# One block for all self-attention scores, and both experts in one strided stationary read

## The chip, the cores and the metric

The kernel runs on one core of a Trainium2 chip. The metric is the device time of one execution in microseconds. Five engines work side by side: TensorE (PE in the profile; its weight loads are listed apart as PEld), VectorE (DVE), ScalarE (ACT), GpSimd (POOL) and SyncE (SP), which issues most of the transfers. TensorE writes to PSUM, which has eight banks of 512 float32 values on each of 128 partitions; the operands of its matmuls lie in SBUF.

## The reference

The input is 16 batches of 128 tokens by 512 values, and for each batch a context of 2048 rows by 512. All is float32.

```python
x = x + xattn(layernorm(x), ctx)     # softmax(h @ ctx.T) @ ctx, over the 2048 rows
x = x + attn(layernorm(x), ...)      # 16 heads of 32, causal, 128 tokens
x = x + ffn(layernorm(x), ...)

# attn: q = [q_c, rope(q_e)], k likewise, v; each projected down to 16 x 64 and up to 16 x 32
scores = einsum("bhqd,bhkd->bhqk", q, k) / sqrt(32)
att = softmax(where(causal, scores, -inf))
y = einsum("bhqk,bhkd->bhqd", att, v) @ Wc

# ffn: two of eight experts for each batch, chosen by its first token
gates = softmax(top2(x[:, 0] @ Wr.T))          # zero for the other six
mid = einsum("blh,erh->belr", x, A)            # rank 64 for each expert
out = x + einsum("be,belr,ehr->blh", gates, mid, Bw)
```

## The kernel before

The 16 batches are worked through one after another, and each has four stages written as generators: `score` (the cross-attention scores and their exponentials), `attend` (those weights times the context), `inner` (the self-attention) and `experts` (the feed-forward part). Each `yield` ends a step. A loop over `b` calls `step(kind, batch, n)` in an order written out by hand, so that steps of four different batches alternate: `inner` of batch b, `experts` of b - 1, `attend` of b + 1, `score` of b + 2. The helpers `matmul` (line 84) and `transpose` (line 87) keep TensorE's instructions in that order. The other engines' instructions are ordered by the scheduler, from what they depend on. Loads in the loop are issued from SP's queue as their buffers come free; the gathers of expert weights and the outputs are issued from POOL.

The names on which the text rests:

- `score`: `psc` is a bank of 512 scores, four for a batch, each from four matmuls of 128 rows with 512 columns; line 214 copies it to `sc` and takes its maximum, and line 223 makes the exponentials of all 2048.
- `attend`: `tr_p` turns four 128 x 128 blocks of `sc` in PSUM, line 120 copies them to `pT` on ACT, and `av` accumulates the product with the context in one bank. Line 247 adds the input. Then a layer norm follows (lines 105 to 112; the power on line 110 is POOL's).
- `inner`: `q`, `k` and `v` are products with weights folded at the start; `tr_q` and `trk` turn q and k. Line 298 makes `kb`, two copies of 128 columns of the turned k, with a mask that leaves one head of 32 partitions in each 64-partition half. `pss` holds the scores of four heads in one bank: a matmul contracts over 64 partitions and gives two heads, 256 columns. Line 316 adds the causal mask, line 322 takes the maxima, line 323 scales them, line 325 makes the exponentials head by head with their sums, and lines 329 and 330 normalise. `tr_p_a` turns the weights, `y` multiplies them with v in 32-column pieces, line 352 copies the result to `yT`, and `o` multiplies that with `Wc`.
- `experts`: DVE works out the two experts from `lg`, POOL gathers their weights to `wa` (two gathers, one row of 1 KB to each partition for each expert, line 400) and `wb` (line 405); `mid` is the first product, line 424 scales it by the gates, and `ffn` is the second product.

PSUM's eight banks are shared out by three pools: `ps_tr` (three, for what is turned), `ps_sc` (two, for `psc` and `pss`) and `ps_acc` (three, for `q`, `k`, `v`, `av`, `y`, `mid`, `o`, `ffn`).

In `inner` of the kernel before, the scores are made in two steps of eight heads. Each takes both banks of `ps_sc`, and steps of `attend` stand between and after the two. Every matmul is two records of the profile.

Of the kernel before, what the change touches and what calls it, by code (L numbers as in the profile page):

```python
# [11 lines left out]
F32 = mybir.dt.float32  # L12
I32 = mybir.dt.int32
U32 = mybir.dt.uint32
AF = mybir.ActivationFunctionType
ALU = mybir.AluOpType
AX = mybir.AxisListType
PSUM = bass.MemoryType.PSUM

P = 128  # L20
B, S, V, D = 16, 128, 2048, 512
H, L, DH = 16, 64, 32
DE = DH // 2
E, R = 8, 64
KC = D // P
VC = V // 512
HC = H // 4
TOP = 2
EPS = 1e-5
SCALE = 1.0 / math.sqrt(DH)  # L30
# [3 lines left out]
C_ID, C_MASK, C_COS, C_SIN, C_BLK = 0, 128, 256, 272, 288  # L34
# [26 lines left out]
def perceiver_block(ctx: ExitStack, tc: tile.TileContext, io: dict, out: bass.AP):  # L61
    nc = tc.nc
# [20 lines left out]
    def matmul(*args, **kwargs):  # L83
        tc.keep_in_program_order(nc.tensor.matmul(*args, **kwargs))  # L84
# [12 lines left out]
    def bank(pool, tag, name):  # L97
        return pool.tile([P, 512], F32, tag=tag, name=name)
# [152 lines left out]
    def inner(b):  # L251

        x1, h = firsts.pop(b)
        hT = p1.tile([P, KC, S], F32, tag="hT2", name=f"hT2_{b}")
        transposed(h, hT, f"2_{b}")
        yield

        qk = p1.tile([P, 2, D], F32, tag="qk", name=f"qk_{b}")
        vv = p1.tile([P, D], F32, tag="vv", name=f"vv_{b}")
        for i, n in enumerate(("q", "k", "v")):  # L260
            ps = bank(ps_acc, "acc", f"{n}_{b}")
            for c in range(KC):
                matmul(ps, hT[:, c, :], w[n][:, c, :], start=(c == 0), stop=(c == KC - 1))
            nc.scalar.copy(vv if n == "v" else qk[:, i, :], ps)
            if n == "k":

                e = qk.rearrange("p i (h f) -> p (i h) f", f=DH)[:, :, DE:]
                turned = p1.tile([P, 2 * H, DE], F32, tag="turned", name=f"turned_{b}")
                for odd in range(2):
                    nc.gpsimd.tensor_tensor(  # L270
                        turned[:, :, odd::2],
                        e[:, :, 1 - odd :: 2],
                        cst[:, None, C_SIN + odd : C_SIN + DE : 2].to_broadcast([P, 2 * H, DE // 2]),
                        ALU.mult,
                    )
                nc.vector.tensor_tensor(
                    e, e, cst[:, None, C_COS : C_COS + DE].to_broadcast([P, 2 * H, DE]), ALU.mult
                )
                nc.vector.tensor_tensor(e, e, turned, ALU.add)
            yield  # L280

        qT = p1.tile([P, HC, S], F32, tag="qT", name=f"qT_{b}")
        transposed(qk[:, 0, :], qT, f"q_{b}")
        trk = bank(ps_tr, "tr", f"trk_{b}")
        for c in range(HC):
            transpose(trk[:, c * P : (c + 1) * P], qk[:, 1, c * P : (c + 1) * P], ident)
        yield
        att = p1.tile([P, H, S], F32, tag="att", name=f"att_{b}")
        nmx = p2.tile([P, H], F32, tag="nmx", name=f"nmx_{b}")
        sm = p2.tile([P, H], F32, tag="sm", name=f"sm_{b}")  # L290
        rsm = p2.tile([P, H], F32, tag="rsm", name=f"rsm_{b}")
        for two in range(2):

            pss = [bank(ps_sc, "sc", f"pss_{b}_{two}_{half}") for half in range(2)]
            kbs = []
            for c in (2 * two, 2 * two + 1):
                kb = p2.tile([P, 2, S], F32, tag="kb", name=f"kb_{b}_{c}")
                nc.vector.tensor_tensor(
                    kb,
                    trk[:, None, c * P : (c + 1) * P].to_broadcast([P, 2, S]),  # L300
                    cst[:, C_BLK : C_BLK + 2, None].to_broadcast([P, 2, S]),
                    ALU.mult,
                )
                kbs.append(kb)

            for i, kb in enumerate(kbs):
                for half, ps in enumerate(pss):
                    of = slice(half * 2 * DH, (half + 1) * 2 * DH)
                    matmul(
                        ps[:, i * 2 * S : (i + 1) * 2 * S],  # L310
                        qT[of, 2 * two + i, :], kb[of].rearrange("p h t -> p (h t)"),
                        start=True, stop=True,
                    )
            for half, ps in enumerate(pss):
                hs = slice(8 * two + 4 * half, 8 * two + 4 * half + 4)
                nc.vector.tensor_tensor(  # L316
                    att[:, hs, :],
                    ps.rearrange("p (h t) -> p h t", h=4),
                    cst[:, None, C_MASK : C_MASK + S].to_broadcast([P, 4, S]),
                    ALU.add,  # L320
                )
                nc.vector.tensor_reduce(nmx[:, hs], att[:, hs, :], AX.X, ALU.max)  # L322
                nc.vector.tensor_scalar_mul(nmx[:, hs], nmx[:, hs], -SCALE)  # L323
                for i in range(hs.start, hs.stop):
                    nc.scalar.activation(  # L325
                        att[:, i, :], att[:, i, :], AF.Exp,
                        bias=nmx[:, i : i + 1], scale=SCALE, accum_out=sm[:, i : i + 1],
                    )
                nc.vector.reciprocal(rsm[:, hs], sm[:, hs])
                nc.vector.tensor_tensor(  # L330
                    att[:, hs, :], att[:, hs, :], rsm[:, hs, None].to_broadcast([P, 4, S]), ALU.mult
                )
            yield

        flat = att.rearrange("p h t -> p (h t)")

        def heads(c):
            first = c // 2 * 8 + c % 2 * 2
            return first, first + 1, first + 4, first + 5

        now = [turn(flat, heads(c), f"a_{b}_{c}") for c in range(HC)]
        yield
        acc = bank(ps_acc, "acc", f"y_{b}")
        for c in range(HC):
            for j in range(4):
                at = c * P + j * DH
                matmul(
                    acc[j * DH : (j + 1) * DH, c * P : (c + 1) * P],
                    vv[:, at : at + DH], now[c][:, j, :], start=True, stop=True,
                )  # L350
        yT = p1.tile([P, HC, S], F32, tag="yT", name=f"yT_{b}")
        nc.scalar.copy(yT, acc.rearrange("p (c t) -> p c t", c=HC))  # L352
        yield
        acc = bank(ps_acc, "acc", f"o_{b}")
        for c in range(HC):
            matmul(acc, yT[:, c, :], w["c"][:, c, :], start=(c == 0), stop=(c == HC - 1))
        x2 = p2.tile([P, D], F32, tag="x2", name=f"x2_{b}")
        nc.vector.tensor_tensor(x2, acc, x1, ALU.add)
        lasts[b] = (x2, layernorm(x2, f"3_{b}"))
        yield  # L360

    def experts(b):
# [50 lines left out]
        nc.vector.tensor_scalar(gate, ex, column(C_TWO), column(C_ONE), ALU.mult, ALU.add)  # L413
        nc.vector.tensor_scalar(gate, gate, dn, None, ALU.mult)
        yield
        ps = bank(ps_acc, "acc", f"mid_{b}")
        for c in range(KC):
            for i in range(TOP):
                matmul(
                    ps[i * R : (i + 1) * R, :S], wa[:, i, c * R : (c + 1) * R], hT[:, c, :],  # L420
                    start=(c == 0), stop=(c == KC - 1),
                )
        mid = p2.tile([P, S], F32, tag="mid", name=f"mid_{b}")
        nc.scalar.activation(mid, ps[:, :S], AF.Copy, scale=gate)
        yield
# [13 lines left out]
    def step(kind, b, n=1):  # L439
        if not 0 <= b < B:  # L440
            return
        if (kind, b) not in gens:
            gens[kind, b] = kind(b)
        for _ in range(n):
            next(gens[kind, b])
# [40 lines left out]
    for b in range(B):  # L486
        if 2 < b + 2 < B:
            load_turned(b + 2)
        step(inner, b, 2)
        step(experts, b - 1)  # L490
        step(score, b + 2)
        step(inner, b)
        step(experts, b - 1)
        step(score, b + 2, 2)
        step(inner, b)
        step(score, b + 2)
        step(attend, b + 1)
        step(inner, b)
        step(attend, b + 1)
        step(inner, b)  # L500
        step(attend, b + 1)
        step(score, b + 2)
        step(attend, b + 1)
        if b == B - 1:

            step(experts, b - 1, 2)
        step(inner, b)
        step(attend, b + 1)
        if b + 2 < B:
            load_ctx(b + 2)  # L510
        if b + 3 < B:
            load_x(b + 3)
        step(inner, b)
        if b < B - 1:
            step(experts, b - 1)
        step(inner, b)
        step(inner, b + 1)
        if b < B - 1:
            step(experts, b - 1)
        step(score, b + 3)  # L520
# [43 lines left out]
```

## Time and profile before

| | |
|---|---|
| median of 3 runs | 910.48 us (910.23 to 912.07) |
| the profiled execution | 910.24 us |
| its span, first to last instruction | 908.5 us |
| mean granted TensorE clock | 0.983 |
| busy: PE, DVE, ACT, POOL | 873.1, 388.6, 291.0, 143.7 us |
| records of `pss`, count and busy time | 256, 38.6 us |
| records of `mid`, count and busy time | 256, 19.9 us |
| weight loads of `mid`, 64 columns, mean | 147 ns |

The span is the time between the first and the last instruction in one profiled execution, and the 1.7 us that are left of its 910.24 us lie around it. A row of the timeline gives the start, the length, the engine, the line, the operation, what it writes and reads, its shapes and how many records were merged. For TensorE, "128*64" before the shapes says that the stationary operand covers 128 rows and 64 columns of the array. The ends of matmuls are modelled, and records that run side by side overlap, so times on TensorE are best read from one start to the next.

### The profile page before, as it was taken

To read this page: it belongs to the slowest core of one execution; us is meant where nothing else is said; L and a number is where in the kernel's file an instruction comes from. 1 tells how busy PE (TensorE), PEld (TensorE's weight loads), DVE (VectorE), ACT (ScalarE), POOL (GpSimd) and SP (SyncE) were. 2 spreads that over 40 slices of the span, in tenths; PEclk is the share of its full clock that TensorE was granted. 3 is DMA by queue.
4 is the path that set the end of the run, shared out by engine and by line. 5 is a ranking of instruction groups with operands and counts; after the bars stand their busy time and mean duration, and the time that the engine had idled before them with its cause. 6 is when DMAs were issued, how large, how long until landed. Compare 5 with 4: busy or idle time off the path is not lost.

```text
span 908.5 us, 10128 instructions
## 1 busy us (share of the span) xinstructions
PE 873.1 (96%) x3600; PEld 445.2 (49%) x3600; DVE 388.6 (43%) x1020; ACT 291.0 (32%) x845; POOL 143.7 (16%) x214
## 2 busy tenths in 40 slices
PE   5999999999999999999999999999999999999972
PEld 2444545555455555545555554555555455555531
DVE  1132535344453534445353444545344454536251
ACT  1132422425142232514233151523315152334240
POOL 0000021120302112030211203021120302112212
PEclk9999999999999999999999999999999999999985
DMA  7997635546273554526356462735545262240011
GB/s 307 365 343 312 238 121 209 208 144 221 90 258 122 209 209 152 219 92 255 117 209 209 155 221 93 251 114 209 208 162 223 89 248 102 73 148 24 12 35 36
DMA packets 29394, 159.21 MB, mean 175 GB/s; under 512 B 4128, under 2 KB 4256, under 8 KB 12960
## 3 DMA queue, kind: packets, MB, share of 16 engines
q1 hardware_dynamic: 25248, 145.98, 43.8%
q0 software_dynamic: 4096, 12.59, 4.0%
q8 instruction: 29, 0.48, 0.2%
q14 instruction: 21, 0.17, 0.1%
HBM read 154.36 MB, written 4.19 MB: 175 GB/s over the span
## 4 chain that ended last, share of the span: by engine, by line
PE 95%; DVE 2%; issue 1%; ACT 1%; POOL 1%; DMA 0%; POOLq 0%; SPq 0%; ACTq 0%
PE av L84 25%; PE psc L84 25%; PE o L84 6%; PE q L84 6%; PE v L84 6%; PE k L84 6%; PE pss L84 4%; PE tr_p_a L87 3%; PE tr_p L87 3%; PE tr L87 2%; PE y L84 2%; PE mid L84 2%; PE ffn L84 1%; PE tr_q L87 1%; PE trk L87 1%
## 5 line engine op out<-in xcount | busy, mean ns | idle before, releaser
L84 PE MATMUL av<-ctx,pT 128*128 128x512 f32 x512 | 233.3, 598 | 0.2 <-ACT pT L120 0.2
L84 PE MATMUL psc<-ctxT,hT 128*128 128x512 f32 x512 | 232.2, 603 | 0.7 <-ACT hT L120 0.7
L84 PEld LDWEIGHTS av<-ctx,pT 128*128 128x128 f32 x512 | 93.4, 190 | 109.9 <-issue 104.8
L84 PEld LDWEIGHTS psc<-ctxT,hT 128*128 128x128 f32 x512 | 95.5, 193 | 104.7 <-issue 103.6
L325 ACT ACTIVATE att<-att,nmx 128x128 f32<-128x128 f32 x256 | 99.0, 388 | 82.7 <-DVE nmx L323 82.7
L214 DVE TENSOR_SCALAR_CACHE_REDUCE sc<-psc 128x512 f32<-128x512 f32 x64 | 44.2, 691 | 133.7 <-PE psc L84 132.8
L109 POOL TENSOR_SCALAR rs<-mv 128x1 f32<-128x1 f32 x48 | 10.4, 229 | 534.6 <-DVE mv L107 534.1
L84 PE MATMUL o<-w_c,yT 128*128 128x512 f32 x128 | 59.2, 605 | 1.5 <-ACT yT L352 1.5
L84 PE MATMUL q<-w_q,hT 128*128 128x512 f32 x128 | 58.8, 602 | 0.7 <-ACT hT L120 0.7
L84 PE MATMUL v<-w_v,hT 128*128 128x512 f32 x128 | 57.6, 592 | 0.0
L84 PE MATMUL k<-w_k,hT 128*128 128x512 f32 x128 | 57.5, 592 | 0.0
L112 DVE TENSOR_SCALAR h<-x,mv,rs 128x512 f32<-128x512 f32 x48 | 39.3, 819 | 39.7 <-POOL rs L110 38.8
L120 ACT COPY pT<-tr_p 128x512 f32<-128x512 f32 x64 | 35.2, 575 | 65.3 <-PE tr_p L87 65.2
L120 ACT COPY hT<-tr 128x512 f32<-128x512 f32 x48 | 27.0, 593 | 80.7 <-PE tr L87 80.7
L247 DVE SCALAR_TENSOR_TENSOR x<-av,rden,x 128x512 f32<-128x512 f32 x16 | 12.0, 750 | 89.5 <-PE av L84 89.5
L325 ACT ACTIVATION_READ_ACCUMULATOR att<-att,nmx 128x1 f32 x256 | 47.7, 186 | 0.0
L330 DVE TENSOR_TENSOR att<-att,rsm 128x512 f32<-128x512 f32 x64 | 44.1, 689 | 1.6
L223 ACT ACTIVATE sc<-sc,nm 128x2048 f32<-128x2048 f32 x16 | 32.0, 2002 | 35.8 <-DVE nm L221 35.8
L400 POOL DMA_INDIRECT wa<-in_A_dram,g_blocks x32 | 32.9, 1028 | 66.4 <-issue 48.5
L87 PEld LDWEIGHTS tr_p<-cst,sc 128*128 128x128 f32 x256 | 30.9, 141 | 24.8 <-issue 24.8
L316 DVE TENSOR_TENSOR att<-pss,cst 128x512 f32<-128x512 f32 x64 | 42.2, 681 | 1.7 <-PE pss L84 1.7
L322 DVE TENSOR_REDUCE nmx<-att 128x4 f32<-128x512 f32 x64 | 40.7, 675 | 0.0
(95 smaller groups left out, 859.1 us busy)
## 6 DMA issues: line engine op xcount, KB each, us to landing
ctxT<-in_ctxT_dram SPq DMA_DIRECT2D x64, 1024.0 KB, 5.1
ctx<-in_ctx_dram SPq DMA_DIRECT2D x64, 1024.0 KB, 4.8
x<-in_x_dram SPq DMA_DIRECT2D x16, 256.0 KB, 4.8
out_dram<-out POOLq DMA_DIRECT2D x16, 256.0 KB, 2.4
down_q<-in_Wq_downT_dram SPq DMA_DIRECT2D x2, 1024.0 KB, 9.5
down_k<-in_Wk_downT_dram SPq DMA_DIRECT2D x2, 1024.0 KB, 7.4
down_v<-in_Wv_downT_dram SPq DMA_DIRECT2D x2, 1024.0 KB, 8.3
w_c<-in_Wc_dram SPq DMA_DIRECT2D x1, 1024.0 KB, 13.5
```

The lines of the kernel that those rows point to most:

```text
L84: tc.keep_in_program_order(nc.tensor.matmul(*args, **kwargs))
L87: tc.keep_in_program_order(nc.tensor.transpose(*args))
L112: nc.vector.tensor_scalar(h, src, mv[:, 0:1], rstd, ALU.subtract, ALU.mult)
L120: nc.scalar.copy(dst, tr.rearrange("p (c t) -> p c t", c=4))
L214: nc.vector.tensor_scalar(sc[:, v * 512 : (v + 1) * 512], ps, 1.0, None, ALU.mult, ALU.max, accum_out=mx[:, v : v + 1],)
L223: nc.scalar.activation(sc, sc, AF.Exp, bias=nm, accum_out=den)
L247: nc.vector.scalar_tensor_tensor(x1, acc, rden, xs.pop(b), ALU.mult, ALU.add)
L316: nc.vector.tensor_tensor(att[:, hs, :], ps.rearrange("p (h t) -> p h t", h=4), cst[:, None, C_MASK : C_MASK + S].to_broadcast([P, 4, S]), ...
L322: nc.vector.tensor_reduce(nmx[:, hs], att[:, hs, :], AX.X, ALU.max)
L325: nc.scalar.activation(att[:, i, :], att[:, i, :], AF.Exp, bias=nmx[:, i : i + 1], scale=SCALE, accum_out=sm[:, i : i + 1],)
L330: nc.vector.tensor_tensor(att[:, hs, :], att[:, hs, :], rsm[:, hs, None].to_broadcast([P, 4, S]), ALU.mult)
L400: nc.gpsimd.indirect_dma_start(wa[:, i, :], None, io["A"], bass.IndirectOffsetOnAxis(ap=blocks[:, i : i + 1], axis=0),)
```

## The change

Self-attention scores: the four `kb` tiles are made one after another ahead of all score matmuls, from a pool of four buffers instead of two. The 16 heads' scores go to four banks that are held together, two of `ps_sc` and two of `ps_acc`. The eight matmuls follow each other in one block, and mask, maxima, exponentials and normalisation of the four groups follow in one step. `inner` has one `yield` less, and the hand-written order loses one step of it: the two steps of `attend` that stood around the second scores block are now next to each other.

The middle product of `experts`: the host lays each expert's `A` with the rank outside and the chunk of the hidden size inside, so that a gathered row of `wa` holds 64 x 4 values rather than 4 x 64. The columns of both experts for one chunk are then every fourth value of the row of 512, and one matmul takes all 128 of them as its stationary operand, 16 bytes apart. Eight matmuls with 64 columns become four with 128.

```diff
-        for two in range(2):
-            pss = [bank(ps_sc, "sc", f"pss_{b}_{two}_{half}") for half in range(2)]
-            kbs = []
-            for c in (2 * two, 2 * two + 1):
-                kb = p2.tile([P, 2, S], F32, tag="kb", name=f"kb_{b}_{c}")
...
-            for i, kb in enumerate(kbs):
-                for half, ps in enumerate(pss):
-                    of = slice(half * 2 * DH, (half + 1) * 2 * DH)
-                    matmul(
-                        ps[:, i * 2 * S : (i + 1) * 2 * S],
-                        qT[of, 2 * two + i, :], kb[of].rearrange("p h t -> p (h t)"),
-                        start=True, stop=True,
-                    )
-            for half, ps in enumerate(pss):
-                hs = slice(8 * two + 4 * half, 8 * two + 4 * half + 4)
...
-            yield
+        kbs = []
+        for c in range(HC):
+            kb = p4.tile([P, 2, S], F32, tag="kb", name=f"kb_{b}_{c}")
...
+        pss = [
+            bank(pool, tag, f"pss_{b}_{tag}_{half}")
+            for pool, tag in ((ps_sc, "sc"), (ps_acc, "acc")) for half in range(2)
+        ]
+        for c, kb in enumerate(kbs):
+            for half in range(2):
+                of = slice(half * 2 * DH, (half + 1) * 2 * DH)
+                matmul(
+                    pss[c // 2 * 2 + half][:, c % 2 * 2 * S : (c % 2 + 1) * 2 * S],
+                    qT[of, c, :], kb[of].rearrange("p h t -> p (h t)"),
                     start=True, stop=True,
                 )
+        for group, ps in enumerate(pss):
+            hs = slice(4 * group, 4 * group + 4)
...
+        yield
...
+        both = wa.rearrange("p i n -> p (i n)")
         ps = bank(ps_acc, "acc", f"mid_{b}")
         for c in range(KC):
-            for i in range(TOP):
-                matmul(
-                    ps[i * R : (i + 1) * R, :S], wa[:, i, c * R : (c + 1) * R], hT[:, c, :],
-                    start=(c == 0), stop=(c == KC - 1),
-                )
+            matmul(ps[:, :S], both[:, c::KC], hT[:, c, :], start=(c == 0), stop=(c == KC - 1))
...
         step(attend, b + 1)
         step(inner, b)
-        step(attend, b + 1)
-        step(inner, b)
-        step(attend, b + 1)
+        step(attend, b + 1, 2)
         step(score, b + 2)
...
-        "A": laid(p["A"].reshape(E, R, KC, P).transpose(0, 3, 2, 1)).reshape(E * P, KC * R),
+        "A": laid(p["A"].reshape(E, R, KC, P).transpose(0, 3, 1, 2)).reshape(E * P, R * KC),
```

More of the change, by code (lines that the diff above doesn't have):

```diff
@@ L291, in inner @@
         rsm = p2.tile([P, H], F32, tag="rsm", name=f"rsm_{b}")
-        for two in range(2):
-            pss = [bank(ps_sc, "sc", f"pss_{b}_{two}_{half}") for half in range(2)]
-            kbs = []
-            for c in (2 * two, 2 * two + 1):
-                kb = p2.tile([P, 2, S], F32, tag="kb", name=f"kb_{b}_{c}")
[L298 to L302, printed above, removed]
-                )
-                kbs.append(kb)
-            for i, kb in enumerate(kbs):
-                for half, ps in enumerate(pss):
-                    of = slice(half * 2 * DH, (half + 1) * 2 * DH)
-                    matmul(
-                        ps[:, i * 2 * S : (i + 1) * 2 * S],
-                        qT[of, 2 * two + i, :], kb[of].rearrange("p h t -> p (h t)"),
-                        start=True, stop=True,
-                    )
-            for half, ps in enumerate(pss):
-                hs = slice(8 * two + 4 * half, 8 * two + 4 * half + 4)
[L316 to L320, printed above, removed]
-                )
[L322 to L327, printed above, removed]
-                    )
[L329 to L332, printed above, removed]
-            yield
@@ new lines, in inner @@
+        kbs = []
+        for c in range(HC):
+            kb = p4.tile([P, 2, S], F32, tag="kb", name=f"kb_{b}_{c}")
+            nc.vector.tensor_tensor(
+                kb,
+                trk[:, None, c * P : (c + 1) * P].to_broadcast([P, 2, S]),
+                cst[:, C_BLK : C_BLK + 2, None].to_broadcast([P, 2, S]),
+                ALU.mult,
+            )
+            kbs.append(kb)
+        pss = [
+            bank(pool, tag, f"pss_{b}_{tag}_{half}")
+            for pool, tag in ((ps_sc, "sc"), (ps_acc, "acc")) for half in range(2)
+        ]
@@ new lines, in inner @@
+        for c, kb in enumerate(kbs):
[4 more added lines that the diff above has]
+                    qT[of, c, :], kb[of].rearrange("p h t -> p (h t)"),
+                    start=True, stop=True,
+                )
+        for group, ps in enumerate(pss):
+            hs = slice(4 * group, 4 * group + 4)
+            nc.vector.tensor_tensor(
+                att[:, hs, :],
+                ps.rearrange("p (h t) -> p h t", h=4),
+                cst[:, None, C_MASK : C_MASK + S].to_broadcast([P, 4, S]),
+                ALU.add,
+            )
+            nc.vector.tensor_reduce(nmx[:, hs], att[:, hs, :], AX.X, ALU.max)
+            nc.vector.tensor_scalar_mul(nmx[:, hs], nmx[:, hs], -SCALE)
+            for i in range(hs.start, hs.stop):
+                nc.scalar.activation(
+                    att[:, i, :], att[:, i, :], AF.Exp,
+                    bias=nmx[:, i : i + 1], scale=SCALE, accum_out=sm[:, i : i + 1],
+                )
+            nc.vector.reciprocal(rsm[:, hs], sm[:, hs])
+            nc.vector.tensor_tensor(
+                att[:, hs, :], att[:, hs, :], rsm[:, hs, None].to_broadcast([P, 4, S]), ALU.mult
+            )
@@ L415, in experts @@
         yield
+        both = wa.rearrange("p i n -> p (i n)")
         ps = bank(ps_acc, "acc", f"mid_{b}")
         for c in range(KC):
-            for i in range(TOP):
-                matmul(
-                    ps[i * R : (i + 1) * R, :S], wa[:, i, c * R : (c + 1) * R], hT[:, c, :],
-                    start=(c == 0), stop=(c == KC - 1),
-                )
+            matmul(ps[:, :S], both[:, c::KC], hT[:, c, :], start=(c == 0), stop=(c == KC - 1))
         mid = p2.tile([P, S], F32, tag="mid", name=f"mid_{b}")
```

## The prediction

> **What bounds the kernel now.** I read the engine shares first, then the chain that ended last, then one batch as a stage window, then TensorE's timeline in it.
>
> ```profile
> PE 873.1 (96%) x3600; PEld 445.2 (49%) x3600; DVE 388.6 (43%) x1020; ACT 291.0 (32%) x845; POOL 143.7 (16%) x214
> ...
> PE 95%; DVE 2%; issue 1%; ACT 1%; POOL 1%; DMA 0%; POOLq 0%; SPq 0%; ACTq 0%
> ```
> ```profile
> 303.70:356.50 52.80, 52.80 (x217) 27.11 (x216) 23.95 (x64) 17.59 (x53) 8.94 (x13) 1.00 0.49 179
> ```
>
> The window's columns are its length and the busy time of PE, weight loads, DVE, ACT and POOL, then clock, DMA share and GB/s. One batch repeats every 52.9 us, and PE is busy in all of this stretch; the list of PE's waits has no entry in this stretch. The other engines are under half busy and DMA at 49%. So the inner batches last as long as PE's own work, and the question is what each block of matmuls costs there. [...]
>
> ```profile
> 306.81 1.04 PE L87 MATMUL tr_p<-cst,sc 128*128 128x128 f32 x8
> 307.78 1.14 PE L84 MATMUL pss<-kb,qT 64*128 64x256 f32 x8
> 308.84 3.70 PE L84 MATMUL av<-ctx,pT 128*128 128x512 f32 x8
> 312.38 0.60 PE L87 MATMUL tr_p<-cst,sc 128*128 128x128 f32 x4
> 312.91 1.13 PE L84 MATMUL pss<-kb,qT 64*128 64x256 f32 x8
> 313.98 3.70 PE L84 MATMUL av<-ctx,pT 128*128 128x512 f32 x8
> 317.51 0.60 PE L87 MATMUL tr_p<-cst,sc 128*128 128x128 f32 x4
> 317.95 3.60 PE L84 MATMUL psc<-ctxT,hT 128*128 128x512 f32 x8
> 321.38 3.60 PE L84 MATMUL av<-ctx,pT 128*128 128x512 f32 x8
> 324.82 1.99 PE L87 MATMUL tr_p_a<-cst,att 128*128 128x128 f32 x16
> ...
> 330.17 1.08 PE L84 MATMUL y<-pT_a,vv 128*32 128x128 f32 x32
> 331.18 1.10 PE L84 MATMUL mid<-hT,wa 128*64 128x128 f32 x16
> 332.21 3.70 PE L84 MATMUL o<-w_c,yT 128*128 128x512 f32 x8
> 335.75 0.60 PE L87 MATMUL tr<-cst,h 128*128 128x128 f32 x4
> ```
>
> [...] Undisturbed prices: eight av records 321.38 to 324.82 = 3.44, so 0.43 for 512 columns; four tr_p before psc 317.51 to 317.95 = 0.44, so 0.109 for 128 columns; by the same rate 0.215 for 256. Now the same groups beside a block of another tile shape (the "64*128" and "128*64" in the rows):
> - eight tr_p before pss take 0.97 instead of 0.87: +0.10;
> - eight pss are four pairs, one of each 64-row half side by side: 4 x 0.215 = 0.86, but 1.06 pass: +0.20;
> - av after pss takes 3.54 instead of 3.44: +0.10.
>
> A pss block costs 0.40 us over its work. For mid, eight pairs of 128 columns are 0.87, 1.03 pass (+0.16), and o after it takes 3.54, not 3.44 (+0.10).
>
> [...] the excess stands only at changes of shape, about 0.1 us each, with the first weight load exposed on top. [...]
>
> ```profile
> L84 PEld LDWEIGHTS k<-w_k,hT 128*128 128x128 f32 x128 | 24.3, 190 | 30.6 <-issue 30.6
> L84 PEld LDWEIGHTS y<-pT_a,vv 128*32 128x32 f32 x512 | 12.9, 109 | 11.7 <-issue 11.5 <-ACT pT_a L120 0.2
> ```
>
> 128 against 32 columns is (190 - 109) / 96 = 0.84 ns a column, 0.108 us for 128. [...] No weight load of this trace reads with a stride[...]. The nearest row is on DVE: L378 reads 32 elements from two operands with strides of 32 and 512 bytes.
>
> ```profile
> 888.60 0.21 DVE L378 TENSOR_TENSOR g_share<-w_r,hT 128x32 f32<-128x32 f32 x1 [1.43 <-ACT hT L120]
> 888.85 0.19 DVE L384 TENSOR_REDUCE g_part<-g_share 128x8 f32<-128x32 f32 x1
> ```
>
> It takes 0.02 us more than a contiguous pass over 32 elements, at most 0.7 ns an element. That is a small penalty or a large part of a doubling; it decides little.
>
> **The change, part by part.**
>
> *Scores in one block.* Two pss blocks a batch become one of 16 records, in four banks. The eight pairs remain; one block's excess goes: -0.40 us. The second block vanishes from between tr_p and av_1, two like shapes, so nothing replaces it. This holds for batches 0 to 14, where attend of the next batch runs around it: 15 x 0.40 = 6.0 us.
>
> What moves: the four kb products (0.38 us each) run together after trk. They start at 303.58 and end near 305.1, while PE is in psc until 306.8; covered. The two extra banks come from ps_acc, which q, k and v have left by 296.2 (vv copied at 295.61 for 0.58), so no wait there. y, mid and o then take banks read by the mask additions and by L247, the first by about 313, 17 us before y. The kb pool grows by two buffers of 1 KB a partition. No DMA is moved or added on any queue, SP's or POOL's.
>
> ACT's order changes: sixteen exponentials (0.385 apart) now stand ahead of the copies of pT_2 and pT_3. They start at 311.53 as now. Masking, maxima and scaling of the third and fourth groups wait on DVE, behind which stand the first normalisation too; adding its rows (0.65 to 0.69 each, ten of them from 308.94, 0.16 to 0.18 for the small ones) gives about 315.2 for the third group's bias, 0.6 us after ACT has finished two groups. So the exponentials end near 318.3 and pT_2 near 318.9. PE reaches av_2, which reads it, at about 321.0 by the new sum (307.78 + 1.92 for pss + 3.54 + 0.44 + 3.43 + 0.44 + 3.43). Margin 2 us: no cost. The last normalisation ends near 319.3, tr_p_a starts near 324.4: no cost.
>
> *Mid as one product.* Sixteen records with 64 columns in side-by-side pairs become eight with 128. Before: mid to the end of o is 1.03 + 3.54 = 4.57. After: call c the time per weight load. The first is exposed, since y has another shape before it; each of eight loads then paces its matmul, if c is at least 0.109[...]: 8c + 0.11 + 3.43. With c = 0.109, its matmul's own time, this is 4.41, -0.16; fourteen batches (mid_0 to mid_13) make -2.2 us. The price is unknown because the columns lie 16 bytes apart[...]. Bounds: c = 0.109 [...], c = 0.214 if it doubles: 5.25, +0.68, or +9.5 over fourteen. A gain beyond 0.16 is excluded, as eight times 128 columns must still stream. I take 0.109 to 0.12, about -1.7 us. o needs yT: its copy runs 331.32 to 331.90 and o would start at 332.16; covered, by 0.25. mid now waits for both wa gathers; they were issued by 300, 30 us before: covered.
>
> *The end.* In batch 15 the scores are on the path, PE waiting for DVE to free the two banks. kb_2 and kb_3 move ahead of the first mask (+0.1). Then ACT's gap before its third group (started at 873.21) shrinks, by the same DVE addition, to 872.7: about -0.4 together. mid_15 at the end has 14 records after its second gather, 895.85 to the copy at 897.91; eight loads at half clock take the same 2 us: 0.
>
> Sum: -6.0 - 1.7 - 0.4 = -8.1 us. The profiled execution took 910.24 (span 908.5 and 1.7 around it), 0.24 under the median 910.48: 902.1 against 902.4. I give 902.5.
>
> **The rivals.**
> 1. *The strided load is slow* (slower). [...] 9.5 - 6.0 - 0.4, plus 1.7 for mid_15 at half clock, is +4.8: 915. It decides from c = 0.18: there 8 x 0.18 + 3.54 - 4.57 = 0.41 cancels the 0.40. For it: [...] L378's excess. Against it: a float32 column leaves 0.84 ns, and only 128 columns are read. Three times as slow (0.32) would give +22.
> 2. *Half-way.* c = 0.165 to 0.195: both edits cancel, 909 to 912. Nothing in the trace excludes it.
> 3. *Softmax comes late.* The 2 us before av_2 vanish, because DVE's interleaving holds ACT longer than I add up. Each further microsecond costs 15 a run; 3 us late instead of 2 early, +7: 917. Against it: ACT's work is unchanged and ends earlier than its 320.5 of now.
> 4. *The merged block saves less:* [...] The eight records in two banks today show 0.40 of excess in all; if the half inside the block returned, 15 x 0.20 = 3 us are lost: 905.
>
> **How the numbers follow.** No change, for this kernel, is within 0.2%, 1.8 us. Free or nearly free stride with the full or half saving of the block: 0.58, own range 901 to 905.5. A mild penalty (c 0.13 to 0.165), 905 to 908.5: 0.05. Rival 2: 0.10. Rival 1: 0.24. Rival 3: 0.03. Faster 0.63, same 0.10, slower 0.27. The range goes from 900.5, the sum with all of 0.16 and a little more at the end, to 916, past a doubled load.
>
> **What would show it.** Right: one pss block of 16 records lasting 1.92, no second; tr_p x4 to av_1 in 0.44; mid of 8 records about 1.0 from start to o, o in 3.44; a batch every 52.35 us; weight loads of mid near 190 ns. Wrong: weight loads of mid at 300 ns with mid taking 1.8 us or more (rival 1), an ACT release in front of av or tr_p_a (rival 3), a pss block over 2.1 us (rival 4).

## The result, and the profile after

The changed kernel takes 918.88 us (median of 4 runs, 917.1 to 920.48) against 910.47 us: a ratio of 1.0081, 95% interval 1.0061 to 1.0101. It is slower by 0.8%. The forecast of 902.5 was wrong, and the time lies above the forecast's range too. Its profiled execution took 918.69 us, with a span of 916.9. The page's engine shares, and one batch as a stage window (columns as in the prediction):

```profile
PE 877.8 (96%) x3472; PEld 461.0 (50%) x3472; DVE 384.4 (42%) x1020; ACT 291.5 (32%) x845; POOL 143.7 (16%) x214
```
```profile
303.70:357.04 53.34, 53.34 (x209) 28.19 (x208) 23.75 (x63) 17.70 (x52) 8.94 (x14) 1.00 0.49 178
```

PE has 128 records fewer and is busy longer. It is still busy through all of a batch, but a batch now lasts 53.34 us instead of 52.89: the bound is the same and its work has grown by 0.45. The timeline of PE shows where:

```profile
309.39 1.04 PE L87 MATMUL tr_p<-cst,sc 128*128 128x128 f32 x8
310.36 1.13 PE L84 MATMUL pss_sc<-kb,qT 64*128 64x256 f32 x8
311.32 1.03 PE L84 MATMUL pss_acc<-kb,qT 64*128 64x256 f32 x8
312.28 3.70 PE L84 MATMUL av<-ctx,pT 128*128 128x512 f32 x8
315.82 0.60 PE L87 MATMUL tr_p<-cst,sc 128*128 128x128 f32 x4
316.26 3.60 PE L84 MATMUL av<-ctx,pT 128*128 128x512 f32 x8
...
332.35 1.08 PE L84 MATMUL y<-pT_a,vv 128*32 128x128 f32 x32
333.36 2.13 PE L84 MATMUL mid<-hT,wa 128*128 128x128 f32 x8
335.33 3.60 PE L84 MATMUL o<-w_c,yT 128*128 128x512 f32 x8
338.77 0.60 PE L87 MATMUL tr<-cst,h 128*128 128x128 f32 x4
```

The scores block starts at 310.36 and av at 312.28: 1.92 us, to the digit of the sum. The second block's place is gone: tr_p x4 goes to av in 0.44. This half of the change gains 0.40 us a batch. From its start to o, mid takes 1.97 instead of 1.03, and o after it 3.44 instead of 3.54: 5.41 for 4.57, so 0.84 is lost. 0.84 - 0.40 is the 0.45 of a batch, to rounding. The weight loads of mid say why:

```profile
L84 PEld LDWEIGHTS mid<-hT,wa 128*128 128x128 f32 x128 | 31.1, 327 | 11.5 <-issue 11.5
```

A load of 128 columns lasts 327 ns here, and 189 to 193 for the contiguous weights of q, k, v, o, av and psc. After the first, the single loads start 0.233 us apart in the trace, and the matmuls with them.

From the first q to the last, the profiled executions differ by 6.88 us (785.22 less 778.34): thirteen batches of +0.45, batch 0 at -0.40 (no mid stands in it), and batch 14 at +1.42. Most of the rest of the span's 8.4 lies ahead of the edits: the first q starts at 75.28 instead of 73.66, before anything that was edited has run on PE. In the runs below that start lies between 73.7 and 75.3, in no visible relation to the edit, so one execution can differ from another by up to 1.6 us for this alone.

Batch 14 is odd by one wait:

```profile
839.16 3.60 PE L84 MATMUL av<-ctx,pT 128*128 128x512 f32 x8
842.60 0.60 PE L87 MATMUL tr_p<-cst,sc 128*128 128x128 f32 x4
843.89 3.70 PE L84 MATMUL av<-ctx,pT 128*128 128x512 f32 x8 [0.69 <-ACT pT L120]
```

From tr_p to av 1.29 us pass where 0.44 would do. There is no batch 16, so no psc stands ahead of this av, and ACT copies pT only after all sixteen exponentials, the last of which ends at 843.3.

### The profile page after: what moved, and what is told of

The parts are those of the page before. It is cut to its first block, busy times and chain, and to the rows that moved or that the text cites. A ratio compares the mean times of both kernels' runs of the same rounds, so it can differ in the third digit from the quotient of the medians.

```text
span 916.9 us, 9886 instructions
## 1 busy us (share of the span) xinstructions
PE 877.8 (96%) x3472; PEld 461.0 (50%) x3472; DVE 384.4 (42%) x1020; ACT 291.5 (32%) x845; POOL 143.7 (16%) x214
## 4 chain that ended last, share of the span: by engine, by line
PE 93%; ACT 1%; DMA 1%; DVE 1%; issue 1%; POOL 0%; SPq 0%; POOLq 0%; ACTq 0%
PE psc L84 24%; PE av L84 24%; PE q L84 6%; PE o L84 6%; PE v L84 6%; PE k L84 6%; PE tr_p_a L87 3%; PE mid L84 3%; PE tr_p L87 3%; PE tr L87 2%; PE pss_sc L84 2%; PE y L84 2%; PE ffn L84 2%; DMA x<-in_x_dram 1%; PE pss_acc L84 1%
## 5 line engine op out<-in xcount | busy, mean ns | idle before, releaser
L84 PE MATMUL mid<-hT,wa 128*128 128x128 f32 x128 | 34.3, 413 | 8.3 <-DMA wa<-in_A_dram,g_blocks 8.3
L87 PE MATMUL tr<-cst,h 128*128 128x128 f32 x192 | 27.7, 279 | 14.7 <-DVE h L112 14.7
```

Source lines behind the costliest of these rows:

```text
L87: tc.keep_in_program_order(nc.tensor.transpose(*args))
```

## The experiments

The theory was now: the strided weight load is all of the loss, and the scores block gains what was forecast. The first four runs take the two edits apart.

**The scores alone.** mid and the layout of `A` are those of the kernel before; the scores are changed.

```diff
-            matmul(ps[:, :S], both[:, c::KC], hT[:, c, :], start=(c == 0), stop=(c == KC - 1))
+            for i in range(TOP):
+                matmul(
+                    ps[i * R : (i + 1) * R, :S], wa[:, i, c * R : (c + 1) * R], hT[:, c, :],
...
```

> The changed scores alone; mid is the pairs of 64 contiguous columns of the kernel before. Theory (the strided weight load is all of the loss, the scores block saves its two changes of shape): batches every 52.49 us (52.89 - 0.40), one wait of 0.7 us for pT before av in batch 14 as in the changed kernel, so 14 x 0.40 - 0.6 = -5.0 us and near -0.4 at the end: 904.5 to 906. Rival (the block loses elsewhere, in a late softmax or other banks): no less than 909, with releases by ACT or DVE before TensorE blocks.

Measured: 906.11 us, ratio 0.9945 (0.9933 to 0.9957). Batches are 52.49 us apart, exactly 0.40 less, and the wait of 0.69 in batch 14 is there. The theory holds, though the time lies 0.1 above the range that it gave; the rival asked for 909 or more.

**The strided product alone.** Scores as before, mid and the layout of `A` as changed.

> The strided middle product alone; the scores are in two blocks as before. Theory: each of its eight weight loads takes 0.233 us, mid and the o after it together 5.41 instead of 4.57, batches every 53.73 us, fourteen of them: +11.8, so 921 to 923. Rival (the two edits disturb each other, or the wait for both gathers costs): under 917, with mid's loads below 0.2 us apart.

Measured: 924.23 us, ratio 1.0144 (1.0127 to 1.0160). Batches are 53.73 apart, +0.84, as the theory has it. The time lies above the 921 to 923 that it gave; the kernel before had a median of 911.38 beside it, not 910.48, which makes up for most of that. The two edits are independent: -0.40 and +0.84 add up to the changed kernel's +0.45.

**The softmax in two steps again,** with the score matmuls still in one block:

```diff
-        yield
+            if group % 2:
+                yield
...
-        step(attend, b + 1, 2)
+        step(attend, b + 1)
+        step(inner, b)
+        step(attend, b + 1)
```

> As the scores-only kernel (one block of score matmuls, contiguous mid), but the softmax of the four groups is again two steps, with a step of attend between them. Theory (in batch 14 nothing stands between tr_p and av_2, so pT, copied behind all sixteen exponentials, is late): the copy of pT_2 moves ahead of the last eight exponentials, the release by ACT before av in batch 14 goes, and the time is 0.6 to 0.8 us under the scores-only kernel's; the batches stay 52.49 us apart. Rival (that wait is covered by a later one): no difference, another wait of 0.7 us follows in that batch.

Measured: 905.13 us, ratio 0.9935 (0.9921 to 0.9949). Batch 14 in the scores-only kernel and then in this one:

```profile
830.37 0.60 PE L87 MATMUL tr_p<-cst,sc 128*128 128x128 f32 x4
831.65 3.70 PE L84 MATMUL av<-ctx,pT 128*128 128x512 f32 x8 [0.69 <-ACT pT L120]
```
```profile
831.01 0.60 PE L87 MATMUL tr_p<-cst,sc 128*128 128x128 f32 x4
831.45 3.60 PE L84 MATMUL av<-ctx,pT 128*128 128x512 f32 x8
```

The wait is gone and batch 14 is 0.95 us shorter (38.60 from its q to the next, against 39.55), somewhat more than the 0.6 to 0.8 expected. The medians differ by 1.0, but the intervals overlap: the mechanism is shown, its worth in the whole time is not.

**The columns side by side.** One matmul for both experts, two-step softmax, `A` laid as before, but POOL copies the gathered weights so that the 128 columns touch. Batches 14 and 15 keep the pairs of 64.

```diff
+        if b < B - 2:
+            side = p2.tile([P, KC, TOP * R, 1], F32, tag="side", name=f"side_{b}")
+            for i in range(TOP):
+                nc.gpsimd.tensor_copy(
+                    side[:, :, i * R : (i + 1) * R, 0],
+                    wa[:, i, :].rearrange("p (c r) -> p c r", c=KC),
+                )
...
+                matmul(
+                    ps[:, :S], side[:, c, :, 0], hT[:, c, :],
...
```

> As the two-step kernel, and for batches 0 to 13 POOL copies the gathered weights of both experts side by side (a tile of 4 chunks x 128 columns), so mid is four matmuls of 128 contiguous columns. Theory (the stride alone makes the load slow): mid's loads come 0.109 us apart, mid to the end of o is 4.41 instead of 4.57, 14 x 0.16 = 2.2 us less than the two-step kernel: about 902. Rival (128 columns cannot load under 128 streamed columns of a float32 pass, stride or not): loads 0.2 us apart and no gain over the two-step kernel, or a loss. Second rival (POOL's copies hold up DVE or the layer norms): releases by POOL or DVE before tr, over 905.

Measured: 902.82 us, ratio 0.9909 (0.9893 to 0.9924). Of this run, PE's timeline and the loads:

```profile
330.33 1.16 PE L84 MATMUL mid<-hT,side 128*128 128x128 f32 x8
331.32 3.60 PE L84 MATMUL o<-w_c,yT 128*128 128x512 f32 x8
334.76 0.60 PE L87 MATMUL tr<-cst,h 128*128 128x128 f32 x4
```
```profile
L84 PEld LDWEIGHTS mid<-hT,side 128*128 128x128 f32 x112 | 13.6, 191 | 2.8 <-issue 2.8
```

mid takes 0.99 and o 3.44: 4.43, near the 4.41 of the forecast. The same eight records with the same shapes take 0.98 us less when their columns are 4 bytes apart and not 16, so the rival falls. (The columns also come from another tile here; the runs below keep that tile and change the distance alone.) Batches are 52.36 apart, and PE has no wait in the inner ones, so the second rival falls too.

**How the load depends on the stride.** Three runs on the mechanism. They are the regrouped kernel with a one-step softmax and a wider pitch, `[P, KC, TOP * R, 2]`, then 3, and for 32 bytes 8 (two chunks interleaved in one buffer, which POOL fills with eight copies). Theories A to E are in the expectations.

> As the kernel with the scores block and POOL's regrouping (one softmax step), but the 128 columns of a chunk lie 8 bytes apart[...]. Theory A [...]: loads 0.109 us apart, as contiguous. Theory B (any stride halves the rate): 0.2 us or more, as in the changed kernel's 0.233. Theory C [...]: about 0.17.

> As the 8-byte kernel, with columns 12 bytes apart[...]. Theory A [...]: between 0.109 and 0.233, nearer the latter. Theory D (the limit is strides of 16 bytes and more, as such): 0.109. Theory B: 0.2 or more.

> As the 8-byte kernel, with columns 32 bytes apart. Theory A and D [...]: 0.233 us as with 16 bytes. Theory E (the price grows with the distance[...]): well over 0.25.

mid and the o behind it, from the timelines of the 8-, 12- and 32-byte kernels, in this order:

```profile
329.56 1.21 PE L84 MATMUL mid<-hT,side 128*128 128x128 f32 x8
330.61 3.60 PE L84 MATMUL o<-w_c,yT 128*128 128x512 f32 x8
```
```profile
330.47 1.66 PE L84 MATMUL mid<-hT,side 128*128 128x128 f32 x8
331.96 3.60 PE L84 MATMUL o<-w_c,yT 128*128 128x512 f32 x8
```
```profile
333.44 2.17 PE L84 MATMUL mid<-hT,side 128*128 128x128 f32 x8
335.44 3.60 PE L84 MATMUL o<-w_c,yT 128*128 128x512 f32 x8
```

Here c is read from the starts of single loads, after the first; with it the forecast's form, 8c + 0.11, gives mid to o to about 0.01. The fourth column is c divided by the distance. The first row is the two-step kernel above; with one step, below, mid to o and c are the same and the time is 901.14. The times of the 8-, 12- and 32-byte rows are of one execution each:

| stride | mid to o, us | c, us | c per byte of distance, ns | time of the run, us |
|---|---|---|---|---|
| 4 bytes | 0.99 | 0.112 | 28.0 (c is near the matmul's own 0.109) | 902.82 |
| 8 | 1.05 | 0.118 | 14.8 | 903.86 |
| 12 | 1.49 | 0.173 | 14.4 | 909.89 |
| 16 (the change) | 1.97 | 0.233 | 14.6 | 918.88 |
| 32 | 2.00 | 0.238 | 7.4 | 918.21 |

In these five kernels c grows with the distance from 8 to 16 bytes, by 14.4 to 14.8 ns for each byte of it; at 16 bytes that is 1.82 ns a column. At 4 bytes it stays near the 0.109 in which 128 columns stream, and 32 bytes cost hardly more than 16. None of the theories had this whole. B falls at 8 and 12 bytes (0.118 and 0.173, not 0.2 or more), D at 12 (0.173, not 0.109) and E at 32 (0.238, not well over 0.25); C's 0.17 for 8 bytes is too much. A's numbers were near on 8, 12 and 32 bytes, but the load at 8 bytes is already 0.118 and not 0.112. Why c grows so, and where between 16 and 32 bytes it stops, no run shows.

**64 columns, 16 bytes apart.** The changed scores and the changed layout, but mid in pairs: `wa[:, i, c::KC]`.

> The changed scores, and mid as before in pairs of 64 columns side by side in the array, but from the changed layout, 16 bytes apart. By the changed kernel's 1.82 ns for a column (0.233 / 128), 64 columns take 0.117 us. If the two loads of a pair run side by side with the stride too: pairs 0.117 to 0.12 us apart against 0.109, mid 1.08 us instead of 1.03, batches 52.55 us. If strided loads share one path: pairs 0.233 us apart, mid about 2.0 us, batches 53.5 us.

Measured: 907.01 us, batches 52.62 apart, mid 1.15 from start to o:

```profile
330.03 1.23 PE L84 MATMUL mid<-hT,wa 128*64 128x128 f32 x16
331.18 3.70 PE L84 MATMUL o<-w_c,yT 128*128 128x512 f32 x8
```

After the first, the trace has the pairs 0.120 us apart (0.109 with contiguous columns), as the first branch says. Sixteen loads with a mean of 208 ns (147 in the kernel before) start within mid's 1.15 us, so the two of a pair run side by side with the stride too. mid is longer than the expected 1.08 because the first pair, whose load nothing hides, takes 0.22 instead of 0.16. The stride costs 0.13 a batch there and 0.98 in one load of 128.

**The moving operand.** Changed scores, contiguous pairs of weights, and hT of the experts' stage laid `[P, S, KC]`, so that its 128 columns are 16 bytes apart.

> The changed scores and the contiguous pairs of 64 weight columns, but the moving operand of mid (hT of the experts' stage) is laid with its 128 columns 16 bytes apart; ACT writes it so from PSUM. By the law that the weight loads show ([...] 0.118 us at 8 bytes, 0.174 at 12, 0.234 at 16), if it is one of reading SBUF and not of loading weights: [...] pairs 0.233 us apart instead of 0.109, mid 2.0 us or more, batches 53.5 us. If only weight loads pay: pairs 0.109 us apart and batches 52.49 us, as with the scores alone.

Measured: 918.09 us, batches 53.41 apart, and of its timeline:

```profile
332.45 2.02 PE L84 MATMUL mid<-hT,wa 128*64 128x128 f32 x16
334.40 3.70 PE L84 MATMUL o<-w_c,yT 128*128 128x512 f32 x8
```

mid takes 1.95, a little under the expected 2.0, with its pairs 0.228 us apart: 1.78 ns a column. So the price is not one of loading weights alone; a streamed operand pays nearly the same. It is not a limit that all reads share, either: the two strided loads of a pair ran side by side above, in 0.120 us, where one load of 64 columns at 1.82 ns a column would take 0.117. Which part of the path from SBUF sets the price, no run here shows.

**Regrouped, softmax in one step.**

> As the regrouped kernel (902.8), with the softmax in one step as the change has it. Theory (the late pT of batch 14 costs 0.6 to 1 us whatever mid does): batches 52.36 us, the release by ACT before av in batch 14 back, 903.3 to 904. Rival (which of the two is ahead is set by the end of the kernel, not by batch 14): no more than 902.8.

Measured: 901.14 us, ratio 0.9899 (0.9883 to 0.9915). The 903.3 to 904 of the theory did not come. Batch 14 has its wait and is 0.95 longer (39.42 against 38.47), yet the median is below the two-step kernel's, as the rival has it. In the two profiled executions the stretch after the last q makes up for the wait (55.54 us against 56.59), and the first q start at 73.74 and 75.17; neither is shown to follow from the edit. The intervals overlap widely, so which of the two is ahead isn't settled. Both beat the kernel before and the change.

## Why the prediction was wrong, point by point

- **The bound** was read rightly: PE is busy throughout the inner batches in every trace here, and each kernel's time follows its batch.
- **The scores block** was right in size and mechanism: 0.40 us a batch, 1.92 for the block. Rival 4, the 0.20 inside the block coming back with the second two banks, did not occur: the first pair in the new banks starts 0.216 after the last in the old ones, as the pairs on either side of it do, and the four banks cost one entry and one exit.
- **The step that failed** is the choice of c in the middle product, "I take 0.109 to 0.12": it measured 0.233. The prediction let 128 columns 16 bytes apart load at the pace of contiguous ones, and so gave mid a gain of 0.07 to 0.16 us a batch where 0.84 was lost. The form of the sum held. With 0.233 it gives 8 x 0.233 + 3.54 = 5.40, and 5.41 was measured; with contiguous columns it gives a batch of 52.35, and 52.36 was measured. That pace was an estimate of mine, from the 0.84 ns that a contiguous float32 column takes; no weight load of the kernel before reads with a stride, so its trace did not show c. The runs show 1.82 ns for a column 16 bytes apart.
- **The DVE row** was set aside: "it decides little". Its 0.7 ns an element, put on top of the 0.84 ns of a column, would have given 1.54 ns and c = 0.20, above the 0.18 from which the change loses. That would have had the right sign by luck: the row compares two different operations, and no run shows that the two engines share a price.
- **Rival 1** was right that the strided load is slow, with c a little low (0.214, an estimate: about twice the 0.108 of contiguous columns, and no trace showed the doubling), which made its 4.8 us too small: +0.84 instead of +0.68 a batch is 2.2 us more. Its 1.7 us for mid_15 at half clock did not come: from mid_15's first matmul to the copy 2.30 us pass, where the kernel before took 2.06 after its second gather. Here are the clock of that stretch (0.50, the third column from the end) and the matmuls in it, and then the kernel before:

```profile
904.30:906.50 2.20, 2.14 (x8) 1.94 (x8) 0.00 (x0) 0.00 (x0) 0.00 (x0) 0.50 0.41 119
904.36 2.21 PE L84 MATMUL mid<-hT,wa 128*128 128x128 f32 x8 [6.19 <-DMA wa<-in_A_dram,g_blocks]
```
```profile
895.85 1.97 PE L84 MATMUL mid<-hT,wa 128*64 128x128 f32 x14 [0.52 <-DMA wa<-in_A_dram,g_blocks]
```

The strided loads start 0.233 us apart here too, as at full clock, while the contiguous pairs go from 0.109 to 0.213. So at half clock the stride costs little (0.233 for 128 columns against 0.213). The change passed the range's top of 916 through the larger c (2.2), batch 14 (1.0), the later first q (1.6) and the missing gain at the end (0.4), less those 1.7: with rival 1's 915 that is 918.5.

- **Rival 2**, c between 0.165 and 0.195, was passed: 0.233 lies above it.
- **Rival 3** came true in one batch of fifteen. The 2 us margin held where psc stands before av_2 (in the batch of the window above the copies of pT start at 320.39 and av_2 at 323.57), and I costed all fifteen batches by that order. In batch 14 psc is missing, and the wait with its exposed load costs 0.98 (39.55 of the scores-only kernel, less 38.97 - 0.40).
- **The end** was put at -0.4; from the last q to the end the change took 56.43 us against 56.47. The granted clock there differs among the executions: 0.60 in 8.6 us of the scores-only kernel's, for example, against 0.88 in 10 us at a similar place in that of the kernel before. The ends scatter from 55.4 to 57.3 over the kernels run. Which part is the change's is not known.
- **Two sums among the rivals** are off. With c = 0.32 mid loses 1.53 us a batch, 21.4 in all, and less the 6.4 of the rest that is about +15 without mid_15, not +22. And at 15 us for each further microsecond, +7 belongs to a softmax one microsecond past the margin, not three. Neither case came about.

## What to carry to other kernels

Price an operand's read on TensorE by the distance between its columns before merging matmuls through a stride: here 128 columns took 0.118, 0.173 and 0.233 us at 8, 12 and 16 bytes on the stationary side, and 0.228 at 16 on the moving side, against 0.109 for streaming 128 contiguous ones. This was measured on float32 columns 4 to 32 bytes apart (16 on the moving side); other types and wider strides were not run. If columns cannot be laid side by side by the load, an idle engine can do it: two copies on POOL, with 28 us to spare, turned a loss of 0.84 us a batch into a gain of 0.13. And where PE has no waits, count the changes of the array's tile shape: here each cost about 0.1 us and another 0.1 for the first load, which nothing hides (from the last tr_p to the first pss 0.202 passed instead of 0.109, and from the first pair of pss to the second 0.320 instead of 0.216, in the kernel before); one block fewer a batch was worth 0.40.

## What the runs showed of the hardware that was not expected

- The strided weight loads did not follow the granted clock: they start 0.233 us apart at clock 1.00 and at 0.50. Contiguous pairs went from 0.109 to 0.213.
- Past 16 bytes, more distance was nearly free: columns 16 and 32 bytes apart cost 0.233 and 0.238 us.
- Two side-by-side loads of 64 strided columns do not share the limit that slows one load of 128: 0.120 us for a pair, 0.233 for the one, with 128 columns 16 bytes apart in both.
